# First group in two halves with mask products, staged loads, 768-column rows and reused tiles in a four-block stack

## The chip, the cores and the metric

The kernel runs on one core of one Trainium2 chip. The metric is the device time of one execution in microseconds, the median of several runs. All matrix work is in 32-bit floats.

## The reference

The input x is 8 sequences of 1024 rows of 256. Four blocks follow each other, each on the layer norm of x and added to x:

```python
x = x + linear_attention_layer(_layernorm(x))   # own two norms, gelu FFN 256 -> 1024 -> 256
x = x + relu_ffn(_layernorm(x))                 # 256 -> 1024 -> 256
x = x + softmax_attention(_layernorm(x))        # one head of 256, not causal
x = x + fp4_ffn(_layernorm(x))                  # silu(gate) * up, 256 -> 704 -> 256
```

The first block's attention has 16 heads of 16 columns and is causal. With q and k after a sigmoid, it computes per head and position

```python
sink_in  = normal / sum_d((q + EPS) * (cumsum(k) + EPS))
src_out  = normal / sum_d((k + EPS) * (cumsum(q) + EPS))
cons_sink = sum_d((q + EPS) * (cumsum(k * src_out) + EPS)) / normal
cons_src  = exp(clip(sum_d((k + EPS) * (cumsum(q * sink_in) + EPS)) / normal, -1, 1))
src_comp  = cons_src / cumsum(cons_src) * normal
x = (q * sink_in / normal) @ cumsum(outer(k, v * src_comp)) * sigmoid(cons_sink)
```

`normal` is the position from 1. In block 4 every 16 columns of the activations and weights are scaled by their largest size and rounded to the values of a 4-bit float before each product.

## The kernel before

**Tiling.** The rows are handled in chunks of 128, and four chunks (512 positions) make a group; a sequence has two groups, so there are 16 groups and 64 chunks. `linear_group` (L750) does the attention of block 1 for a group: `front` norms each chunk's x and turns it into `n0T`; q and k come as four tiles of 128 x 512 with columns of heads on the partitions; running sums along positions are scans on VectorE (`running`, L697), with the last column kept in `carry_cur` or `carry_w` for the next group. `head_sums` (L663) adds the 16 columns of each head with products against `hsum`, so that the four kinds of sum of all heads lie packed in one 128 x 128 tile (four chunks of 32 rows). On it the reciprocals and the exponential are done. To multiply q or k by such a packed factor it has to be repeated over the 16 columns of each head: `spread` (L678) writes the packed tile to DRAM and reads it back with each row repeated 16 times, one 128 x 512 tile for each of four parts. This is done for `flow` (four parts) and for `scale` (two parts, of q alone). `linear_chunk` (L897) then does v, the scores, the sum with the carried state `kv_sum`, the product with Wo, and the norm that gives h.

`dense` (L1070) runs both FFNs of a group half by half (256 rows), eight steps of 128 hidden columns each: a first product `half,w_ff`, the activation, and two steps later the second product `w_ff,hidden` into an accumulating bank. Each step's weights (two transfers of 128 KB) are loaded anew into five `w_ff` buffers. `norms_1` and `norms_2` follow each half. When all eight chunks of a sequence are through, `soft_chunk` (L1225) does blocks 3 and 4 for a chunk: the query product with `wqk`, scores against all keys (`n2T,qT`), exponential, transposes, product with `vt`, norm, rounding (`fp4`, L523), gate and up products (`wgT`, `wuT`), silu, rounding of the 704 columns of `hid`, six transposes (`hqT`) and the down product with `wdT`. The 704 columns are five tiles of 128 and one of 64:

```python
INTER_TILES = [(t * P, min(P, INTER - t * P)) for t in range((INTER + P - 1) // P)]
...
                lhsT=hqT[k // 4][:rows_, k % 4, :],
                rhs=wdT[:rows_, k, :],
```

**Order.** All parts are generators that say what they need next. The class `Plan` keeps an estimated time for each engine, tile, buffer and PSUM bank (`took`, L140, has the prices), and `run` (L231) always takes the part that could go on first, TensorE's work last among equals, then by due time (`at`). Every instruction is chained to the one before it on its engine (`Queue`, L255), so the order of this plan is the order on the chip, on all five engines. Times in the plan are not waited for on the chip: there an instruction waits for its operands and buffers alone. Because every instruction is issued through `Queue`, all have line L268 in the profile.

**Buffers.** `TILES` (L42) has the number of buffers of each kind: five `lin`, nine `flow`, seven `prob`, five `soft`, four `rows`, three `hid` and so on. [...]At most four chunks are in `soft_chunk` at a time, and at most two between their query product and their value product.

**Start.** Constants are made first, then the five `v_pad` tiles are cleared, four x chunks are loaded, then all weights and bias rows in one row on the sync engine's queue. The rounding of block 4's weights (`fp4_weights`: `w_raw`) and the product of block 3's query and key weights (`softmax_weights`: `wqk_raw`, `wqk_T`) are started at once and take turns with the first group.

Of the kernel before, what the change touches and what calls it, by code (L numbers as in the profile page):

```python
# [33 lines left out]
BANKS = 8  # L34
INTER_TILES = [(t * P, min(P, INTER - t * P)) for t in range((INTER + P - 1) // P)]
# [9 lines left out]
    "lin": (5, D, F32),  # L45
# [7 lines left out]
    "hid": (3, INTER, F32),  # L53
    "q_c": (2, INTER, BF16),
}


class Plan:
# [9 lines left out]
    def __init__(self, tc, nc):  # L68
        self.tc, self.nc = tc, nc
        self.free = {}  # L70
        self.done = {}
        self.by = {}
        self.banks = []
        self.live = {}
        self.slots = {}
        self.kind = {}
        self.used = {}
        self.held = set()
        self.kept = set()
        self.last = {}  # L80
        self.act_set = 0
        self.parts = []
        for name in ("tensor", "vector", "scalar", "gpsimd", "sync"):
            setattr(self, name, Queue(self, name))
# [19 lines left out]
    def take(self, kind, tile_):  # L104
        name = tile_.tensor.name
        slots, live = self.slots.setdefault(kind, []), self.live.setdefault(kind, set())
        if len(live) + len(slots) == TILES[kind][0]:
# [11 lines left out]

    def slot_free(self, kind):  # L120
        slots, live = self.slots.get(kind, []), self.live.get(kind, ())
        if len(live) + len(slots) < TILES[kind][0]:
            return 0.0
        return min(slots) if slots else None

# [5 lines left out]

    def bank_free(self, tag, n, count):
        banks = self.banks.get(tag, [])
        if len(banks) + count <= n:
            return 0.0
        times = sorted(self.used[b] for b in banks if b not in self.held)
        k = count - (n - len(banks)) - 1
        return times[k] if k < len(times) else float("inf")

    def took(self, queue, op, args, kw):  # L140
# [12 lines left out]
        if queue == "tensor":  # L153
# [4 lines left out]
            if op == "matmul" and (kw["lhsT"].shape[-1] <= 32 or kw["lhsT"].shape[0] <= 32):  # L158
                cost *= 0.25
            after = 0.2  # L160
        elif queue == "vector":
            each = {"reciprocal": 6.2e-3, "tensor_tensor_scan": 2.15e-3}.get(op, 1.05e-3)
            cost = 0.15 + each * size
        elif queue == "scalar":
            cost = 0.2 + 0.95e-3 * size
# [4 lines left out]
        elif queue == "gpsimd":  # L170
            cost = 0.4 + 1.3e-3 * size
        else:
            cost, after = 0.4, 2.2
# [7 lines left out]
        end = start + cost  # L181
        self.free[queue] = end
# [11 lines left out]
    def need(queue, tiles, banks=0, when=None, at=None, unused=(), fresh=None):  # L194
# [3 lines left out]
            queue=queue, tiles=tiles, banks=banks, when=when, at=at, unused=unused, fresh=fresh  # L198
# [14 lines left out]
    def ready(self, need):  # L213
# [8 lines left out]
        if need.fresh is not None:  # L222
            times.append(self.slot_free(need.fresh))
# [7 lines left out]
    def run(self):  # L231
        while self.parts:
            now = self.free.get("tensor", 0.0)
            best = None
            for part in self.parts:
# [3 lines left out]
                key = max(t - now, 0.0), part[1].queue == "tensor", part[2]  # L239
                if best is None or key < best[0]:  # L240
                    best = key, part
            assert best is not None, "every part waits for another"
            if best[0][0] > 0.0:
                self.free["tensor"] = now + best[0][0]
# [42 lines left out]
def block_stack_kernel(ctx: ExitStack, tc: tile.TileContext, a: dict, out: bass.AP):  # L287
# [51 lines left out]
    def make(kind, name=None):  # L339
        bufs, width, dtype = TILES[kind]  # L340
        t = wk.tile([P, width], dtype, tag=kind, name=name or kind, bufs=bufs)
# [11 lines left out]
    def load_row(name, width):  # L353
        t = const.tile([P, width], F32, tag=f"b_{name}", name=f"b_{name}")
        nc.sync.dma_start(out=t, in_=a[name].partition_broadcast(P))
        return t

    def load_tiles(name, width, kt):
        t = const.tile([P, kt, width], F32, tag=f"w_{name}", name=f"w_{name}")
        nc.sync.dma_start(out=t, in_=a[name].rearrange("(k p) n -> p k n", p=P))  # L360
        return t

    def load_cols(name, n):
        t = const.tile([P, n], F32, tag=f"c_{name}", name=f"c_{name}")
        nc.sync.dma_start(out=t, in_=a[name])
        return t


    ident = const.tile([P, P], F32, name="ident")
    make_identity(tc.nc, ident)  # L370
    triu = const.tile([P, P], F32, name="triu")
    make_upper_triangular(tc.nc, triu)
    bdiag = const.tile([P, P], F32, name="bdiag")
    make_block_diagonal(tc.nc, bdiag, DH)
    parity = const.tile([P, 2], F32, name="parity")
    nc.vector.tensor_reduce(
        parity, bdiag.rearrange("p (g e d) -> p e g d", e=2, d=DH), AX.XY, ALU.max
    )
    neghalf = const.tile([P, 1], F32, name="neghalf")
    nc.vector.memset(neghalf, -0.5)  # L380
    one = const.tile([P, 1], F32, name="one")
    nc.vector.memset(one, 1.0)

    hsum = const.tile([P, 4, 32], F32, name="hsum")
    nc.vector.memset(hsum, 0.0)
    for b in range(4):
        nc.vector.tensor_copy(
            hsum[:, b, 8 * b : 8 * b + 8], bdiag.rearrange("p (h d) -> p h d", d=DH)[:, :, 0]
        )

    pos_i = sm.tile([P, P], I32, tag="e", name="pos_i", bufs=1)
    for t in range(G):
        nc.gpsimd.iota(
            pos_i[32 * t : 32 * t + 32, :], pattern=[[1, P]], base=t * P + 1, channel_multiplier=0
        )
    pos = const.tile([P, P], F32, name="pos")
    nc.vector.tensor_copy(pos, pos_i)
    rpos = const.tile([P, NG, P], F32, name="rpos")
    for g in range(NG):
        nc.vector.tensor_scalar(rpos[:, g, :], pos, float(g * GT), None, ALU.add)  # L400
    nc.vector.reciprocal(rpos, rpos)
    row_i = const.tile([P, 1], I32, name="row_i")
    nc.gpsimd.iota(row_i, pattern=[[0, 1]], base=0, channel_multiplier=1)
    nc.vector.tensor_scalar(row_i, row_i, 16, None, ALU.bitwise_and)
    src = const.tile([P, 1], F32, name="src")
    nc.vector.tensor_copy(src, row_i)
    nc.vector.tensor_scalar(src, src, 1.0 / 16.0, None, ALU.mult)
    sink = const.tile([P, 1], F32, name="sink")
    nc.vector.tensor_scalar(sink, src, -1.0, 1.0, ALU.mult, ALU.add)
    sign = const.tile([P, 1], F32, name="sign")  # L410
    nc.vector.tensor_scalar(sign, src, 2.0, -1.0, ALU.mult, ALU.add)
    upper = const.tile([P, 1], F32, name="upper")
# [1007 lines left out]
```

## Time and profile before

| what | us |
|---|---|
| runs: median (lowest to highest of 3) | 2755.65 (2754.45 to 2756.18) |
| profiled execution, its own time | 2750.45 |
| its span, first to last instruction | 2748.6 |
| PE busy | 2614.9 (95%) |
| DVE busy | 1953.3 (71%) |
| ACT busy | 1219.6 (44%) |
| POOL busy | 597.7 (22%) |

The span is what the page's shares refer to; the execution's own time adds 1.85 us. PE is TensorE's products and transposes, DVE is VectorE, ACT is ScalarE, POOL is GpSimd, SP the sync engine that issues all transfers. A 32-bit product[...] stands twice in the counts of PE; a transpose stands once. Ends of matmuls are modelled, so that what a product costs is better read from the start of one to the start of the next.

### The profile page before, as it was taken

The numbers are of one execution on the slowest core, as the hardware profiler recorded it, in microseconds if no ns is written. First come the engines' busy times: TensorE is split into PE (matmuls) and PEld (weight loads), VectorE is DVE, ScalarE is ACT, GpSimd is POOL, SyncE is SP. The second block draws the span as 40 slices with busy tenths as digits, with TensorE's granted clock in tenths as the row PEclk, the third lists the DMA queues.
The fourth block names the chain that finished last, engine by engine and source line by source line (L and its number), as shares of the span: only waits on it lengthen the run. The fifth ranks groups of instructions, "written<-read, shape, count | busy, mean of one in ns | idle before, by whom it ended". The sixth has DMA issues, their size and how long they took to land.

```text
span 2748.6 us, 45646 instructions
## 1 busy us (share of the span) xinstructions
PE 2614.9 (95%) x16620; PEld 1998.1 (73%) x16620; DVE 1953.3 (71%) x4459; ACT 1219.6 (44%) x2453; POOL 597.7 (22%) x1100
## 2 busy tenths in 40 slices
PE   3888999999999999999999999999999999999997
PEld 1667677777777777777777777777777777877664
DVE  6877676685867778587776858768685777755565
ACT  2424344534554454444535354444545445353343
POOL 1323322121321312122221223213131222211000
PEclk7999999999999999999999999999999999999999
DMA  4234231322223232232222223222322313122000
GB/s 107 76 103 141 71 104 57 93 71 86 82 68 98 65 92 67 75 102 62 90 66 78 82 79 100 62 90 69 90 65 80 109 49 91 60 80 76 14 12 14
DMA packets 283215, 211.61 MB, mean 77 GB/s; under 512 B 23921, under 2 KB 270705, under 8 KB 282993
## 3 DMA queue, kind: packets, MB, share of 16 engines
q1 hardware_dynamic: 282992, 208.71, 25.5%
q8 instruction: 133, 2.18, 0.3%
q14 instruction: 90, 0.73, 0.1%
HBM read 189.74 MB, written 18.87 MB: 76 GB/s over the span
## 4 chain that ended last, share of the span: by engine, by line
PE 83%; DVE 11%; DMA 2%; ACT 2%; issue 1%; POOL 1%; SPq 0%; DVEq 0%; POOLq 0%; ACTq 0%
PE bank L268 83%; DVE hid L268 3%; DVE n L268 1%; DVE x_amax L268 1%; DVE ln_st L268 1%; DMA spread<-packed 1%; DVE mx L268 1%; DVE sc L268 1%; DVE prod L268 1%; ACT L268 1%; DMA w_ff<-in_L_ffn_w_dram 1%; SPq L268 0%; DVE u L268 0%; DVE x_r L268 0%; POOL ln_rstd L268 0%
## 5 line engine op out<-in xcount | busy, mean ns | idle before, releaser
L268 PE MATMUL bank<-half,w_ff 128*128 128x256 f32 x2048 | 533.8, 384 | 17.1 <-DMA w_ff<-in_L_ffn_w_dram 13.7
L268 PE MATMUL bank<-w_ff,hidden 128*128 128x256 f32 x2048 | 530.4, 384 | 3.4 <-ACT hidden L268 3.4
L268 PEld LDWEIGHTS bank<-half,w_ff 128*128 128x128 f32 x2048 | 382.8, 192 | 94.9 <-issue 32.3
L268 PEld LDWEIGHTS bank<-w_ff,hidden 128*128 128x128 f32 x2048 | 366.9, 191 | 76.4 <-issue 29.6
L268 ACT ACT_TABLE_LOAD x285 | 365.7, 1283 | 61.9 <-PE bank L268 54.6
L268 POOL TENSOR_SCALAR ln_ve<-ln_mv 128x1 f32<-128x1 f32 x384 | 102.4, 267 | 1110.1 <-DVE ln_mv L268 1099.6
L268 ACT ACTIVATE hidden<-bank,c_L_ffn_b 128x256 f32<-128x256 f32 x256 | 120.8, 472 | 320.5 <-PE bank L268 319.8
L268 PE MATMUL bank<-n2T,qT 128*128 128x512 f32 x512 | 243.9, 599 | 2.3 <-ACT qT L268 2.3
L268 POOL TENSOR_TENSOR ln_rstd<-ln_ve,neghalf 128x1 f32<-128x1 f32 x384 | 237.4, 618 | 32.0
L268 PE MATMUL bank<-vt,probT 128*128 128x256 f32 x1024 | 232.2, 380 | 0.0
L268 DVE TENSOR_TENSOR hid<-hid,bank 128x352 f32<-128x352 f32 x128 | 65.9, 518 | 229.4 <-PE bank L268 189.2
L268 PEld LDWEIGHTS bank<-vt,probT 128*128 128x128 f32 x1024 | 194.0, 190 | 38.1 <-issue 7.7
L268 DVE TENSOR_TENSOR sc<-bank,triu 128x512 f32<-128x512 f32 x256 | 162.3, 682 | 54.9 <-PE bank L268 54.9
L268 PE MATMUL bank<-wdT,hqT 128*128 128x256 f32 (+1 forms) x768 | 190.9, 390 | 0.8 <-ACT hqT L268 0.8
L268 ACT ACTIVATE hidden<-bank,c_L_attn_b 128x256 f32<-128x256 f32 x256 | 121.5, 474 | 146.3 <-PE bank L268 144.8
L268 POOL TENSOR_TENSOR xr<-xr,b_L_attn_ln_b 128x256 f32<-128x256 f32 x64 | 62.6, 996 | 531.3 <-DMA xr<-in_L_attn_inputs_dram 531.1
L268 PE MATMUL bank<-wgT,xqT 128*128 128x352 f32 x512 | 175.4, 465 | 1.4 <-ACT xqT L268 1.4
L268 PE MATMUL bank<-wuT,xqT 128*128 128x352 f32 x512 | 172.4, 459 | 0.0
L268 PEld LDWEIGHTS bank<-wdT,hqT 128*128 128x128 f32 (+1 forms) x768 | 139.7, 190 | 40.8 <-issue 20.2
L268 PEld LDWEIGHTS bank<-n2T,qT 128*128 128x128 f32 x512 | 92.7, 191 | 73.7 <-issue 62.5
L268 PEld LDWEIGHTS bank<-wuT,xqT 128*128 128x128 f32 x512 | 97.3, 190 | 54.1
L268 ACT ACTIVATE hid<-bank 128x352 f32<-128x352 f32 x128 | 59.3, 463 | 154.0 <-PE bank L268 152.6
(174 smaller groups left out, 4382.5 us busy)
## 6 DMA issues: line engine op xcount, KB each, us to landing
w_ff<-in_L_attn_W_dram SPq DMA_DIRECT2D x512, 128.0 KB
w_ff<-in_L_ffn_w_dram SPq DMA_DIRECT2D x512, 128.0 KB
spread<-packed SPq DMA_DIRECT2D x96, 256.0 KB
x<-in_L_attn_inputs_dram SPq DMA_DIRECT2D x64, 128.0 KB
xr<-in_L_attn_inputs_dram SPq DMA_DIRECT2D x64, 128.0 KB
rows<-res SPq DMA_DIRECT2D x64, 128.0 KB
rows<-rows SPq DMA_DIRECT2D x64, 128.0 KB
out_dram<-y SPq DMA_DIRECT2D x64, 128.0 KB
```

Of the source, the lines that this page charges most:

```text
L268: ins = method(*args, **kw)
```

## The change

The first group (p = 0) is computed as two spans of two chunks; all later groups have one span of four. In a span of two the spread is made by TensorE: the packed tile is multiplied with a mask of zeros and ones, and q and k are multiplied with the result in PSUM. The masks are made by ScalarE from the identity, in two `prob` buffers that are free at that time. Loads and constants are put in stages: x of the first two chunks, Wk and Wq come first; rows, FFN weights and block 3's and 4's weights come after the plan has reached a stage (`count["stage"]`). Block 4's rows get 768 columns with zeros at the end. After the last chunk of linear attention, `prob`, `soft` and `rows` tiles can also come from `flow`, `lin` and `x` buffers, q and k become two more `hid` buffers, eight chunks may be in `soft_chunk` instead of four, and three instead of two between query and value product. `lin` has four buffers instead of five. The state product of a chunk shares the bank of its attention product. The plan's prices are changed for all queues, a change of TensorE's tile shape gets a price, and a transfer's landing follows from its bytes; among parts that could go at once, the plan stays with small tiles when the last product was one of these.

```diff
+INTER_PAD = -(-INTER // P) * P
...
-    "lin": (5, D, F32),
+    "lin": (4, D, F32),
...
-    "hid": (3, INTER, F32),
+    "hid": (3, INTER_PAD, F32),
...
+SPARE = {"prob": "flow", "soft": "lin", "rows": "x"}
...
+            if tiled != self.tiled:
+                cost += 0.2
+            self.tiled = tiled
...
-            cost, after = 0.4, 2.2
+            cost = 0.4
...
+        if queue == "sync":
+            n = 4e-6 / 160e-3
+            for d in outs[0].shape:
+                n *= d
+            self.free["rings"] = max(self.free.get("rings", 0.0), end) + n
+            after = self.free["rings"] - end + 1.8
...
-                key = max(t - now, 0.0), part[1].queue == "tensor", part[2]
+                stays = self.tiled and part[1].tiled
+                wait = max(t - now - (0.3 if stays else 0.0), 0.0)
+                key = wait, part[1].queue == "tensor", not stays, part[2]
...
+    def load_weights_and_rows():
+        for i, (stage, label, t, src) in enumerate(loads):
+            yield dma(at=0.0, when=lambda: count["stage"] >= stage)
+            nc.sync.dma_start(out=t, in_=src)
...
+    xs = {c: load_x(c) for c in range(2)}
+    for i in (1, 0):
+        nc.sync.dma_start(out=wqkv[i], in_=wqkv_in[i])
...
+    def spread_near(packed, span, pairs):
+
+        yield pe(packed, *mask_tiles, banks=len(pairs))
+        out = {}
+        for pair in pairs:
+            bank = mm_bank()
+            for j, b in enumerate(pair):
+                mask = mask_tiles[b // 2][:, b % 2 * D : (b % 2 + 1) * D]
+                h = 32 * span.start
+                for t in range(2):
+                    nc.tensor.matmul(
+                        bank[:, j * D + t * P : j * D + (t + 1) * P],
+                        lhsT=mask[h : h + 64, t * P : (t + 1) * P],
+                        rhs=packed,
+                        start=True,
+                        stop=True,
+                    )
+                out[b] = bank[:, j * D : (j + 1) * D]
+            plan.keep(bank)
+        return out
...
+        spans = (range(0, 2), range(2, 4)) if p == 0 else (range(G),)
+        for span in spans[1:]:
+            plan.start(linear_span(p, span, fronts, tiles), p + 0.01)
+        yield from linear_span(p, spans[0], fronts, tiles)
...
-        weighted = yield from spread(flow, (2, 0, 3, 1))
+        if near:
+            weighted = yield from spread_near(flow, span, ((2, 0), (3, 1)))
+        else:
+            weighted = yield from spread(flow, (2, 0, 3, 1))
...
+        yield pe(when=lambda: count["linear"] == B * NCH)
+        plan.spare = True
+        for n in ("q", "k"):
+            h = kept([P, 2, GT], n, 1).rearrange("p k t -> p (k t)")
+            nc.gpsimd.memset(h[:, INTER:INTER_PAD], 0.0)
+            hids.append(h[:, :INTER_PAD])
+        plan.size["hid"] += 2
...
-            for k, (f0, rows_) in enumerate(tiles):
-                nc.tensor.transpose(bank[:rows_, k, :], hid[:, f0 : f0 + rows_], ident)
+            bank = turned([hid[:, f0 : f0 + P] for f0, _ in tiles])
...
-                lhsT=hqT[k // 4][:rows_, k % 4, :],
-                rhs=wdT[:rows_, k, :],
+                lhsT=hqT[k // 4][:, k % 4, :],
+                rhs=wdT[:, k, :],
...
-                when=lambda: q["normed"] == NCH and cc - count["out"] < 4 and "softmax" in weights,
+                when=lambda: q["normed"] == NCH and cc - count["out"] < (8 if plan.spare else 4) and "softmax" in weights and "ends" in late,
```

## The prediction

> **What bounds the kernel now.** I read the slices of the page first, because they say where the idle time lies.
>
> ```profile
> PE   3888999999999999999999999999999999999997
> PEclk7999999999999999999999999999999999999999
> ```
>
> TensorE is the bound, in order and nearly full, except in the first four slices of 68.7 us and the last. The busy time by stage puts numbers on this (columns: stage and its length, then busy us and instructions of PE, PEld, DVE, ACT, POOL, then clock, DMA share, GB/s).
>
> ```profile
> 0.00:100.00 100.00, 44.80 (x441) 30.54 (x445) 66.90 (x168) 22.36 (x58) 16.98 (x43) 0.81 0.31 83
> 100.00:200.00 100.00, 86.96 (x669) 69.03 (x665) 79.26 (x181) 39.37 (x91) 28.62 (x53) 0.95 0.37 112
> 200.00:300.00 100.00, 85.85 (x577) 68.87 (x569) 77.54 (x187) 37.79 (x87) 28.49 (x52) 0.93 0.38 112
> 300.00:400.00 100.00, 95.84 (x667) 74.12 (x656) 66.93 (x144) 45.05 (x85) 27.91 (x50) 0.97 0.32 95
> 400.00:2400.00 2000.00, 1988.48 (x12953) 1526.71 (x12951) 1467.39 (x3330) 936.05 (x1858) 461.75 (x838) 1.00 0.26 79
> 2540.00:2748.60 208.60, 175.16 (x725) 120.82 (x723) 122.96 (x279) 76.18 (x155) 10.54 (x22) 0.96 0.04 13
> ```
>
> PE idles 55.2 us in the first 100, 31.4 in the next 300, 11.5 in the 2000 of the middle and 33.4 in the last 208.6, after the last FFN weights. So time is won in two ways only: less PE work anywhere, or less idle time at the start and at the end. The chain of waits says what the start waits for (start, us, what):
>
> ```profile
> 45.56 2.53 DMA packed<-flow
> 48.10 3.77 DMA spread<-packed
> ...
> 70.90 2.44 DMA packed<-scale
> 74.04 4.66 DMA spread<-packed
> ```
>
> These two round trips through DRAM, 6.3 and 7.8 us from issue to the first product, stand in a chain of DVE work on the whole first group. The first FFN matmul comes at 98.07 in the timeline, the group's fourth transposed h at 109.57. The timeline of PE shows the third place, block 4's last product (start, us, form, count), against an ordinary x4 of 0.86 just before it:
>
> ```profile
> 2390.07 1.03 PE L268 MATMUL bank<-half,w_ff 128*128 128x256 f32 x4
> 2390.93 2.95 PE L268 MATMUL bank<-wdT,hqT 128*128 128x256 f32 x12
> 2393.81 0.44 PE L268 MATMUL bank<-ident,n 128*128 128x128 f32 x2
> ```
>
> From start to start the twelve passes take 2.88 us, twelve ordinary ones 3 x 0.864 = 2.59. The groups by form say which two are dear: the last tile has 64 rows.
>
> ```profile
> L268 PE MATMUL bank<-wdT,hqT 64*128 64x256 f32 x128 | 44.5, 428 | 0.0
> ```
>
> And at the very end the last chunk's fp4 work on DVE is bare:
>
> ```profile
> 2731.20 1.35 PE L268 MATMUL bank<-wuT,xqT 128*128 128x352 f32 x4
> 2739.82 1.51 PE L268 MATMUL bank<-ident,hid 128*128 128x128 f32 x6 [7.28 <-DVE hid L268]
> ```
>
> [...]from the start of one matmul to that of the next it is 0.09 us longer where the tile shape changes (0.309 for 0.216; the 0.29 us above is two changes and a pair that doesn't overlap, 0.320). [...]the clock falls to half. The trace agrees: 0.50 in 40 to 60 us, where PE is busy for 3 of 20. [...] ACT_TABLE_LOAD costs: 1.28 us; the page has 285 at a mean of 1283 ns.
>
> **Part A, 768 columns in block 4.** hid, hqT and wdT get zero rows, so all six tiles have 128 rows. Per chunk 2.88 - 2.59 = 0.29 us of PE; 64 chunks: **-18.4 us**. All lies on PE at its bound. Transposes stay six a chunk, and the 64-column one already takes as long as the others (279 ns both). The two hqT copies (263 + 262 ns) become one of 256 columns (370): 10 us off ACT, which is 44% busy, worth nothing. The new memsets (three hid tails, wdT, later two) are on POOL, 22% busy, under 0.2 us each by v_pad's 0.56 for eight times the width; one FFN step behind them covers it.
>
> **Part B, the start.** The first group's four chunks become two spans of two. A span's spread is made by mask matmuls in PSUM; of DMAs, 2 packs and 6 spreads go. I add the DVE order of the changed program, since DVE carries the chain. A 256-wide scan lies between 467 ns (128 wide) and 1.24 us (512): 0.73. So a flow step is 0.73 + 0.15 carry + 0.42 product = 1.33, a weighted one 1.75.
> - Constants, statistics and norms of x 0 and 1: now constants (3.3 to 8.7) come first and n at 10.8; with half of them put off, 7.8.
> - Rest of the constants, statistics of x 2 and 3: 3.0, to 10.8. k and q of the first span come by 10 to 13 (four 0.86 products, 0.47 sigmoids).
> - Four flow steps 5.3 and two norms 0.85: 16.9. Head sums 0.65, reciprocal 0.95, flow 0.3: 18.8.
> - Mask products: 4 matmuls, 8 passes. None is in the trace; the nearest is the 64-row tile, 0.22 for streaming 256 plus 0.1 for a load that doesn't overlap; for 128 columns 0.21, so 1.7 (0.9 if loads overlap[...]): 20.5. This replaces the 6.3 us trip.
> - Four weighted steps and, between them, the second span's flow steps, 7.0 + 5.3: 32.7. Then e, Exp, totals, reciprocals and scale, 5.6: 38.3; scale's products and q x2, then v: 43. Here the old kernel is at 80.
> - Scores of two chunks, attention, the second span's remaining weighted steps and scale, two norms (DVE 20): first FFN matmul at about **63** instead of 98.
> - Two more chunks (eight sc at 0.68, norms, six weight operations; DVE 20): fourth h at about **85** instead of 109.6.
>
> By then PE has done one first and two second FFN steps more than before (+2.6 us), but not six w_raw tiles and the softmax weights (-5): 24.5 - 2.5 = 22. Those weights now fall beside group 0's FFN, where DVE was 79% busy; six tiles at some 2.9 us of DVE are 17 us in a 100-us stretch with 21 free. I take 2 back: **-20 us**, 8 to 32.
>
> Queues: SP issues x 0, x 1, Wk, Wq first (0.47 each); the rows used later and five FFN weight tiles follow in its list, under 3 MB, at the 191 GB/s of the first 20 us some 15 us, so in well before 63. PE's new wait for flow has the second span's last q product and head sums behind it; DVE needs them two steps later. POOL now waits for bo before its res adds; v_pad memsets are behind them, needed at 43. ACT does eight mask copies (0.37) before n0T, between ident (under 3 us) and 8. All covered; if not, up to 3 us. Fourteen more table loads are 18 us on ACT, covered by its 56% idle.
>
> **Part C, the end.** After linear attention, its flow, lin, x, q and k tiles serve block 3 and 4; eight chunks may be under way instead of four. Both orders have ten last products left after the last FFN matmul. What changes is distance: chunk 62's scores were followed by one product (2.9 us) before its probabilities were transposed; now by that, 0.9 of wqk and 1.7 of scores. Exp needs 0.7 + 0.2 + 1.3 + 1.4 = 3.6, so those waits go; the fp4 waits (DVE hid) go in part. The 7.28 above and the closing 3 us stay. Of 33.4 idle, 10.3 stay for certain; of 23 I take **-14** (0 to -23).
>
> **Part D, the middle.** The planner's prices change, so the whole order changes. Changes of tile shape outside block 4: 288 before, 292 now, 0.4 us. Idle is 0.6% there; a gain is at most 11 us. A loss is open: lin has four buffers for five. I take 0, -5 to +12.
>
> **Sum.** 18.4 + 20 + 14 = 52.4. The profiled execution took 2750.45 (span 2748.6 and 1.85 around it), so 2698; the median shown is 5.2 higher, so 2755.65 - 52.4 = **2703**.
>
> **Rivals.**
> 1. *The early start isn't kept.* FFN weights are 256 KB per 1.73 us of PE, 151 GB/s; from 140 to 160 us DMA moved 146, and PE waited 7.21 us for w_ff. If groups 0 and 1 run at the rate of transfers, an earlier start only meets that wall sooner: 2755.65 - 32.4 = 2723. Against it: 31.4 us in 300 is all the idle there was.
> 2. *The end doesn't shorten*, since the last chunk's chain sets it and the deeper lead comes too late: 2755.65 - 38.4 = 2717. For it: the last five PE steps stand in the same order.
> 3. *Slower: lin with four buffers.* v, k, kv, xo, u and h of a chunk share it; a chunk's v then waits for the u or h of the one before, and PE, in order, stands behind v's bank. The price is per chunk, on 60 chunks: above 52.4 / 60 = 0.87 us each the change loses. At 1.3 (POOL's ve and rstd 0.9 and h 0.5): +78 - 52 = +26, 2781. Against: PE waited 1.2 us in all before the Wo products.
> That the change doesn't do what it says: the changed program's list has the 24 mask matmuls and no 64-row wdT; this is excluded.
>
> **How the numbers follow.** Forecast 0.53, first rival 0.18, second 0.20, third 0.09. Likeliest 2703. The bounds of B, C and D, taken independent, are about 18 up or down; rivals 1 and 2 lie inside that, and the upper end goes part of the way to rival 3: 2676 to 2737. A difference of 0.2%, 5.5 us, is what can be told from none: faster 0.90, the same 0.02, slower 0.08 (the third rival but for its cheap end).
>
> **What would show it.** A: wdT x12 in 2.6 us, no 64-row group. B: first half,w_ff near 63, fourth ident,h near 85, no packed in the first 100 us; PE idle in 0 to 400 near 67, not 87. C: the stretch after the last w_ff near 190 us. D: idle in the middle near 12. It is wrong if PE waits for lin's readers, for w_ff beyond 20 us, or for w_raw, or if the mask products take over 4 us a span.

## The result and the profile after

The kernel after takes **2747.74 us** (median of 8 runs, 2744.89 to 2751.26), the kernel before on the same chip 2754.80 (8 runs, 2749.19 to 2756.76): a ratio of 0.9977, 95% interval 0.9967 to 0.9988. It is faster by 7 us where 52 were forecast, and 2747.74 lies 11 us above the range. The profiled execution took 2751.26 (span 2749.6), while the one of before, at 2750.45, was a short one among its runs; so the two traces below differ by only +1.0 us of span, and 8 us of what the medians show aren't in them.

PE's busy tenths in the slices of the page after:

```profile
PE   6988999999999999999999999999999999999897
```

The first slice rose from 3 to 6. The busy time by stage, in the columns that the prediction named, shows what happened later:

```profile
0.00:100.00 100.00, 73.64 (x587) 55.48 (x588) 80.22 (x207) 31.32 (x76) 27.05 (x64) 0.83 0.30 78
100.00:200.00 100.00, 87.79 (x698) 68.44 (x697) 84.12 (x195) 39.53 (x95) 31.68 (x52) 0.95 0.37 106
200.00:300.00 100.00, 90.80 (x718) 71.16 (x717) 86.08 (x213) 36.17 (x92) 27.89 (x55) 0.98 0.38 113
300.00:400.00 100.00, 98.36 (x571) 74.22 (x570) 74.90 (x157) 49.03 (x97) 23.66 (x41) 1.00 0.36 106
400.00:2400.00 2000.00, 1969.14 (x12793) 1523.38 (x12792) 1458.56 (x3293) 954.50 (x1816) 429.71 (x833) 1.00 0.27 78
2540.00:2749.60 209.60, 175.66 (x714) 124.75 (x712) 121.88 (x278) 63.56 (x134) 11.76 (x22) 0.93 0.04 13
```

PE idles 49.4 us in the first 400 instead of 86.5 (67 were predicted), but 30.9 in the middle 2000 instead of 11.5, and 33.9 in the last stage, which is not shorter. The landmarks of the start, from PE's timeline (start, us, form, count), first of the kernel before, then of the kernel after:

```profile
98.07 1.13 PE L268 MATMUL bank<-half,w_ff 128*128 128x256 f32 x4 [0.24 <-ACT half L268]
...
109.57 0.41 PE L268 MATMUL bank<-ident,h 128*128 128x128 f32 x2 [0.85 <-DVE h L268]
```

```profile
75.67 1.03 PE L301 MATMUL bank<-half,w_ff 128*128 128x256 f32 x4
...
94.22 0.38 PE L301 MATMUL bank<-ident,h 128*128 128x128 f32 x2
```

The first FFN product starts at 75.7 instead of 98.1, the transpose of the fourth h at 94.2 instead of 109.6. Block 4's last product, in the same view, takes 2.59 us from start to start, and no tile of 64 rows is left:

```profile
2531.02 2.75 PE L301 MATMUL bank<-wdT,hqT 128*128 128x256 f32 x12
2533.61 1.03 PE L301 MATMUL bank<-w_ff,hidden 128*128 128x256 f32 x4
```

So the edits do locally what they say. The gain is lost to waits. The longest items of PE's waits in the middle (400 to 2400; what PE waited for, then total us, times, longest), first of the kernel before, then of the kernel after:

```profile
PE bank L268 <- DVE u L268: 3.7, 6, 0.6
PE bank L268 <- ACT hidden L268: 3.4, 6, 0.6
...
```

```profile
PE bank L301 <- DVE y L301: 8.6, 7, 1.4
PE bank L301 <- ACT prob L301: 4.5, 6, 0.9
...
PE bank L301 <- DVE res L301: 2.7, 2, 2.2
...
```

One wait of the largest item of after shows how it comes about. The two timelines around it, PE first, then DVE:

```profile
1340.30 1.03 PE L301 MATMUL bank<-w_ff,hidden 128*128 128x256 f32 x4
1342.56 1.13 PE L301 MATMUL bank<-half,w_ff 128*128 128x256 f32 x4 [1.23 <-DVE y L301]
```

```profile
1340.16 1.28 DVE L301 TENSOR_TENSOR_SCAN prod<-one,carry_w,spread 128x512 f32<-128x512 f32 x1
1341.47 0.69 DVE L301 SCALAR_TENSOR_TENSOR prod<-k,prod 128x512 f32<-128x512 f32 x1
1342.08 0.42 DVE L301 TENSOR_TENSOR y<-bank,rows 128x256 f32<-128x256 f32 x1
```

PE wants a PSUM bank that DVE reads in `y`, 0.42 us of work; but DVE works through a group's weighted steps back to back (from 1330 on, with two norms between them), and `y` stands behind the last of them. DVE isn't overloaded (73% busy in the middle, as before). It has the wrong instruction next.

**A table for all runs.** For each trace I split every distance from the start of one matmul to the start of the next into the usual one for that pair of tile shapes (the median in the traces of before and after) and the rest. The first, summed, is PE's own work; the rest is waiting, which includes what products lose at a reduced clock (0.83 granted in after's first 100 us). What lies ahead of the first matmul's start (11.3 us before, 7.0 after) and behind the last one's (3.5 in both) is in neither. Pairs that occur once only make the sums uncertain by 2 to 3 us. Counting the closely packed small products in another way shifts some 20 us from PE's own work into the waits in every row, most of it in the middle, so differences between rows are uncertain by up to 6. The split is that of the profiled execution, which took between 8 us less (e1) and 6 us more (e12) than the median beside it. All times in us.

| kernel | time, median | PE's own work | waits 0-400 | waits 400-2400 | waits after 2400 |
|---|---|---|---|---|---|
| before | 2754.8 | 2554 | 98 | **35** | 46 |
| after | 2747.7 | 2558 | 63 | **62** | 56 |
| e1 part A alone, planned anew | 2768.4 | 2537 | 98 | 58 | 51 |
| e5 part A alone, order kept | 2736.7 | 2537 | 100 | 36 | 46 |
| e9 after without part A, order kept | 2763.4 | 2574 | 60 | 58 | 55 |
| e3 after, five lin | 2748.7 | 2558 | 62 | 63 | 55 |
| e4 after, no reuse at the end | 2757.1 | 2558 | 62 | 63 | 65 |
| e2 after, old prices, old choice | 2728.1 | 2558 | 76 | 48 | 36 |
| e12 e2 without the reuse | 2736.7 | 2558 | 75 | 49 | 49 |
| e6 after, old choice only | 2738.8 | 2556 | 61 | 66 | 46 |
| e7 after, old prices only | 2780.8 | 2554 | 78 | 105 | 39 |
| e10 before, one price 0.16 | 2801.8 | 2556 | 92 | **93** | 43 |
| e11 after, one price 0.16 | 2743.7 | 2553 | 53 | 65 | 56 |
| e16 e2, one price 0.16 | 2766.3 | 2555 | 76 | **80** | 41 |
| e8 e2, no rounding of weights | 2772.5 | 2554 | 70 | 94 | 47 |
| e15 e2, first group in one span | **2720.7** | 2540 | 89 | 44 | 39 |

Each kernel was compared with the kernel before on its own chip, whose median there was 2752.8 to 2754.8.

### The profile page after: what moved, and what is told of

Same layout as the page of the kernel before. It is cut to its first block, busy times and chain, and to the rows that moved or that the text cites. A ratio compares the mean times of both kernels' runs of the same rounds, so it can differ in the third digit from the quotient of the medians.

```text
span 2749.6 us, 45693 instructions
## 1 busy us (share of the span) xinstructions
PE 2631.4 (96%) x16687; PEld 2025.0 (74%) x16687; DVE 1976.4 (72%) x4509; ACT 1235.2 (45%) x2421; POOL 569.9 (21%) x1106
## 4 chain that ended last, share of the span: by engine, by line
PE 63%; DVE 26%; ACT 3%; issue 2%; DMA 2%; POOL 2%; SPq 0%; DVEq 0%; ACTq 0%
PE bank L301 63%; DVE hid L301 4%; DVE prod L301 4%; DVE n L301 3%; DVE ln_st L301 2%; DVE x_amax L301 2%; DVE spread L301 1%; DVE u L301 1%; DVE mx L301 1%; DVE x_r L301 1%; POOL ln_rstd L301 1%; ACT L301 1%; DVE res L301 1%; DVE ln_mv L301 1%; ACT q_c L301 1%
## 5 line engine op out<-in xcount | busy, mean ns | idle before, releaser
L301 PE MATMUL bank<-w_ff,hidden 128*128 128x256 f32 x2048 | 537.1, 385 | 0.3 <-DVE u L301 0.2
L301 POOL TENSOR_SCALAR ln_ve<-ln_mv 128x1 f32<-128x1 f32 x384 | 95.6, 249 | 1599.7 <-DVE ln_mv L301 1589.2
L301 POOL TENSOR_TENSOR ln_rstd<-ln_ve,neghalf 128x1 f32<-128x1 f32 x384 | 230.2, 600 | 32.0
L301 DVE TENSOR_TENSOR hid<-hid,bank 128x352 f32<-128x352 f32 x116 | 59.9, 517 | 224.5 <-PE bank L301 200.0
L301 PE MATMUL bank<-wdT,hqT 128*128 128x256 f32 x768 | 180.6, 386 | 1.3 <-ACT hqT L301 1.3
L301 PEld LDWEIGHTS bank<-wdT,hqT 128*128 128x128 f32 x768 | 147.9, 194 | 24.6 <-ACT hqT L301 2.6
L301 PEld LDWEIGHTS bank<-wuT,xqT 128*128 128x128 f32 x512 | 98.1, 192 | 56.6 <-issue 1.8
L301 PE MATMUL bank<-ident,n 128*128 128x128 f32 x512 | 99.8, 282 | 24.9 <-DVE n L301 19.4
L301 PEld LDWEIGHTS bank<-wgT,xqT 128*128 128x128 f32 x512 | 94.3, 192 | 38.9 <-issue 6.4
```

Of the source, the lines that this page charges most:

```text
L301: ins = method(*args, **kw)
```

## The experiments

**Part A and the order (e1, e5, e9).** Two versions give the kernel before its 128-row tile (the last tile overlaps the one ahead by 64 columns, and their weight rows are zero). e1 has one hqT copy as in after, and its plan comes out reordered; e5 keeps both ACT copies, and with them the order of every engine (POOL alone has one memset more). e9 takes the 128 rows out of after, with its order kept.

```diff
-                lhsT=hqT[k // 4][:rows_, k % 4, :],
-                rhs=wdT[:rows_, k, :],
+                lhsT=hqT[k // 4][:, k % 4, :],
+                rhs=wdT[:, k, :],
...
 # e1 only
-            if half == 0:
-                nc.scalar.copy(hqT[0], bank)
-            else:
-                for k, (f0, rows_) in enumerate(tiles):
-                    nc.scalar.copy(hqT[1][:rows_, k, :], bank[:rows_, k, :])
+            nc.scalar.copy(hqT[half][:, : len(tiles), :], bank)
```

> The kernel before with block 4's sixth tile made of 128 rows and nothing else (the last tile overlaps the fifth by 64 columns, whose rows of wdT are zero; five lin buffers, old plan). If PE's work is the bound all through, 64 x 0.29 = 18.4 us go and it takes about 2736. If the plan's order has a second bound just behind PE, whose waits take the gain back, it stays at 2750 to 2755, with wdT x12 at 2.59 us all the same.

> The kernel before with one edit: the sixth tile of the gated product's down product takes 128 rows (it overlaps the fifth by 64 columns, whose weight rows are zero), written so that the planned order of every engine's instructions is the one of before. TensorE's own work falls by 64 x 0.29 us = 18 us. Theory 'order' (the PE work counts in full where the order stays; it was only a reshuffled order that cost the first such kernel 27 us of waits): 2737 +- 4 us, PE's stalls near those of before. Theory 'second bound' (vector and scalar results stand just behind PE in every order, so PE waits as soon as it gets faster): 2748 or more, the sequence period stays at 323 to 325 us and the waits for DVE and ACT results grow by 10 us or more.

> The kernel after with the sixth tile of the gated product's down product at 64 rows again, the planned order of every engine unchanged. Theory 'the PE work of part A counts in full in this order too, and was not what was lost': 2748 + 18 = 2766 us, +-4. Theory 'in the order of after PE waits for others, so that its work is partly hidden' (PE's waits in 400 to 2400 are twice those of before): +5 to +12, 2753 to 2760.

Measured: e1 **2768.39** (7 runs, ratio 1.0041, 1.0029 to 1.0052), e5 **2736.68** (4 runs, 0.9936, 0.9922 to 0.9951), e9 2763.38 (7 runs, 1.0035, 1.0022 to 1.0047). The same edit is worth -18.1 us in the kept order, +14 in the reordered one (which neither of my two theories for e1 allowed), and its removal from after costs 15.6. PE's own work moves by 17 us each time; in e5 the waits stay as they were, in e1 22 us of new ones come in the middle. Most are in two items of e1's waits from 400 to 2400:

```profile
PE bank L268 <- DVE n L268: 12.8, 6, 2.5
PE bank L268 <- ACT prob L268: 10.8, 17, 1.2
```

A sequence of two groups, which takes 323.7 us from first FFN product to first FFN product before, takes 321.5 in e5: eight chunks at 0.288 less. This also refutes the idea that I had ahead of e5, that a second bound stands right behind PE.

**Buffers and the end (e3, e4, e12).** e3 gives `lin` its fifth buffer back (and takes hid's tail columns to make room). e4 and e12 leave out the reuse at the end and the depth of eight, in after and in e2.

```diff
-        plan.spare = True
-        for n in ("q", "k"):
-            h = kept([P, 2, GT], n, 1).rearrange("p k t -> p (k t)")
-            nc.gpsimd.memset(h[:, INTER:INTER_PAD], 0.0)
-            hids.append(h[:, :INTER_PAD])
-        plan.size["hid"] += 2
```

> The changed kernel with five lin buffers; for room, block 4's tile of 128 rows is made by overlap as in e1, and hid has 704 columns. Theory 2 (lin): 2720 to 2730, the middle's waits gone. Theory 1 (prices and choice): 2743 to 2750, as the changed kernel.

> The changed kernel without the reuse of flow, lin, x, q and k tiles at the end, four chunks under way. If the reuse brings what it was counted for, 2755 to 2762 (the end 10 to 14 us longer). If the end is set by the last chunks' own chain, 2745 to 2750. If the reuse itself costs (deeper lead puts DVE work of later chunks ahead of what PE needs), 2735 to 2742.

> The kernel after with old prices and old choice of the plan (2728 us) and without the reuse of linear attention's tiles at the end, four chunks under way. The plan up to the last linear group is nearly the same, so this shows what the reuse does at the end in this order. If the reuse is the cause of the short end (193 us after the last weight-tile product for 208): 2740 to 2745, the end back at 205 to 210. If the order is the cause: 2728 +- 4.

Measured: e3 2748.66 (15 runs, 0.9976, 0.9968 to 0.9984), the same as after; so four `lin` cost nothing (the order stays nearly the same: 84 of DVE's 4509 places differ). e4 2757.12 (12 runs, 1.0015, 1.0007 to 1.0024): the reuse is worth 9.4 us. e12 2736.73 (4 runs, 0.9943, 0.9928 to 0.9958): it is worth 8.6 in the other order (I had given 2740 to 2745, or 2728 if the order did it). The waits after 2400 fall by 9 to 13 us with it in both pairs, and the middle stays, so this is the reuse itself.

**The plan (e2, e6, e7, e10, e11, e16).** Each has the instructions of the kernel that it changes, but for ACT's table loads and the choice of reused tiles, in another order. e2 has after's edits with both the prices and the choice of before; e6 takes back the choice alone (with it the price of a change of tile shape), e7 the other prices alone. e10, e11 and e16 change one number, in before, after and e2.

```diff
 # e6; in e2 also the prices
-                stays = self.tiled and part[1].tiled
-                wait = max(t - now - (0.3 if stays else 0.0), 0.0)
-                key = wait, part[1].queue == "tensor", not stays, part[2]
+                key = max(t - now, 0.0), part[1].queue == "tensor", part[2]
 # e10, e11, e16
-            cost = 0.15 + each * size
+            cost = 0.16 + each * size
```

> The changed kernel with the old prices and the old choice in the plan. Theory 1, the new prices and the stay at small tiles make an order in which PE waits some 4 us more per sequence (mostly for DVE): this one takes 2712 to 2725, with the middle's idle time back near 12 us. Theory 2, the four lin buffers: no better than 2745, waits as in the changed kernel.

> The kernel after with its new prices in the plan, but the choice between parts as before (no staying on a small tile shape, no 0.2 us for a switch of the tile, TensorE's planned time moved only by a wait). If the choice rule is what costs the kernel after its end: near 2728 us, last weight-tile product near 2534 us and the rest near 193 us, as with old prices and old choice together. If the prices of the engines and transfers are what costs it: near 2748.

> The kernel after with the prices of before for VectorE, ScalarE, GpSimd and transfers, but the new choice between parts and the price of a tile switch. If the prices cost the 20 us: near 2728 us. If the choice costs them: near 2748. If each costs half, both of this pair come near 2738; if any reshuffled order moves the time by so much, the pair does not add up.

> The kernel before with one number of its plan changed: the fixed part of a VectorE price 0.16 instead of 0.15 us. No instruction is added, removed or made longer; only the order in which the parts are put into the queues changes, in some thousand places. Theory 'the order alone is worth tens of us' (the orders seen so far had 35 to 105 us of PE waits between 400 and 2400, and before has the least of them): 2755 to 2785, with more PE waits in the middle than the 35 us of before. Theory 'the order hardly matters; each edit has its own cost': within 5 us of 2755.

> The kernel after with the same number of the plan changed, 0.16 for 0.15 us. Theory 'the order alone is worth tens of us': anywhere between 2725 and 2785, over 5 us from 2748, and the difference lies in PE's waits, not in its work. Theory 'order hardly matters': within 5 us of 2748.

> The kernel after with old prices and old choice (2728 us) and the fixed part of VectorE's price 0.16 instead of 0.15. No instruction is changed. Theory 'the order alone is worth tens of us': over 5 us from 2728, PE's work near 2558 us again and the difference in its waits. Theory 'order hardly matters in this version': within 5 us.

Measured: e2 **2728.1** (4 runs, 0.9900, 0.9884 to 0.9917), e6 2738.75 (0.9937, 0.9920 to 0.9955), e7 2780.83 (1.0100, 1.0083 to 1.0116). Against after, the old choice alone brings 9 us, the old prices alone cost 33, both together bring 20: they don't add, so neither is a cost of its own. And one hundredth of a microsecond in one price moves before by **+48.5 us** to 2801.78 (from 2753.24 on its chip; 4 runs, 1.0175, 1.0160 to 1.0190), e2 by +38 to 2766.28 (1.0052, 1.0032 to 1.0072) and after by -4 to 2743.73 (0.9965, 0.9952 to 0.9977), which is hardly clear of the noise and, by what I had put down for e11, speaks for an order that hardly matters. PE's own work is the same within 5 each time. My range for e10 ended at 2785, too low, and e2 came 3 us above its range. PE is busy for 1948.2 us of e10's middle, against 1988.5 in before. Over all the orders in the table the waits there lie between 35 and 105 us; those of before, and of e5, which keeps its order, are the lowest. An edit that makes the plan choose anew leaves that order. ACT's table loads change with the order too, but not with the time: e10 has 13 more than before and is slower, e16 has 45 fewer than e2 and is slower as well.

**The start (e8, e15).** e15 is e2 with its first group in one span, through DRAM again; the staged loads and late constants stay. e8 is e2 without the rounding of block 4's weights.

```diff
 # e15
-        spans = (range(0, 2), range(2, 4)) if p == 0 else (range(G),)
+        spans = (range(G),)
 # e8
-            yield from fp4(raw, width, rows)
```

> The kernel after with old prices and old choice of the plan (2728 us), with the first group as one span whose spreads go through DRAM again (the staged loads stay). If the two spans with mask products are worth the start: the first FFN product at 90 us or later instead of 74.5, and the time up by 10 to 20, to 2738 to 2748. If the staged loads and constants brought the start: below 2735. Since this too reorders the plan, PE's waits between 400 and 2400 (48 us in the base) have to be read beside it.

> The kernel after with the plan's old prices and old choice, and the rounding of the gated product's weights left out (the raw weights are turned instead: VectorE's share of this weight work is gone, its PE turns stay). Theory 'displaced vector work' (half of the early start is lost between the first and second group because VectorE's weight rounding, moved out of the start, falls into that group's FFN): the time from group 0's first FFN product to group 1's falls from 120 to near 110 us, and the whole by about as much, to near 2718. Theory 'nothing to do with it' (PE's own work and the order of products set this interval): it stays at 117 to 121 us and the whole at 2725 to 2730.

Measured: e15 **2720.70** (4 runs, 0.9879, 0.9862 to 0.9895), the fastest kernel of this study: 27 us faster than after, and 32 below before on the same chip. The first 100 us of e2, then of e15 (columns as above):

```profile
0.00:100.00 100.00, 75.06 (x595) 57.37 (x596) 77.95 (x206) 31.21 (x78) 27.75 (x64) 0.83 0.30 81
```

```profile
0.00:100.00 100.00, 57.18 (x522) 40.36 (x523) 69.00 (x170) 30.51 (x70) 26.57 (x64) 0.81 0.37 97
```

PE is less busy without the spans, and its first FFN product comes later (81.2 for 74.5). Yet e15's timeline has the fourth h at 90.9, ahead of e2 (93.7) and of after:

```profile
81.24 1.13 PE L284 MATMUL bank<-half,w_ff 128*128 128x256 f32 x4 [0.24 <-ACT half L284]
...
90.90 0.38 PE L284 MATMUL bank<-ident,h 128*128 128x128 f32 x2
```

Group 1's first FFN product comes at 193.6 in e15 and 195.9 in e2. So most of the earlier start is there without the spans (17 of e2's 24 us at the first FFN product), and I put it down to the staged loads. The two spans bring 6.8 us at that product, which are gone one group later: they add 15 us of PE busy time (2612.0 against 2596.9 on the pages), 10 of it in the mask products. In this order they pay for nothing; since leaving them out reorders the plan as well, the 7 us between e15 and e2 aren't theirs alone (4 lie in the middle's waits). In before PE waited 8.4 us of the first 100 for `wqk_raw` from DRAM; e15's list of waits there has no such item.

e8 came out at 2772.46 (4 runs, 1.0068, 1.0053 to 1.0083), outside both of its ranges, because its new order waits more in the middle (94 us). Its start still answers the question: DVE is busy for 128 us from 100 to 300 instead of 154 in e2, and group 1's first FFN product comes 123 us after group 0's, instead of 121. So DVE's rounding isn't what stretches this interval (110 in before); what does is open.

**What a bad order waits for (e13, e14, e17, e18).** In e10 the trace shows a wait of 7 us of DVE, and two of PE after it. DVE's timeline, then PE's:

```profile
1865.33 0.29 DVE L268 SCALAR_TENSOR_TENSOR flow<-pos,r 128x128 f32<-128x128 f32 x1
1872.61 0.69 DVE L268 TENSOR_TENSOR spread<-k,spread 128x512 f32<-128x512 f32 x1 [6.99 <-DMA spread<-packed]
```

```profile
1884.67 0.43 PE L268 MATMUL bank<-prod,hsum 128*32 128x128 f32 x8 [2.33 <-DVE prod L268]
1885.02 2.71 PE L268 MATMUL bank<-wgT,xqT 128*128 128x352 f32 x4
...
1903.29 2.08 PE L268 MATMUL bank<-half,w_ff 128*128 128x256 f32 x4 [3.26 <-DVE u L268]
```

DVE's queue has the product with the spread right behind `flow`, so it stands for the whole round trip through DRAM (6.99 us), and all that stands behind it is late. e13 (and its control e14, in before's order) lets the spreads read what the first group packed. e17 (control e18) leaves the transfer out from the fourth group on, so the factors have no effect there. The order of PE, DVE, ACT and POOL is kept in each.

```diff
 # e13, e14
+            flat = firsts[kind] = hbm.tile([32, GT], F32, tag="packed0", name="packed0", bufs=2)
...
-                    tensor=flat.tensor,
-                    offset=flat.offset + 8 * b * GT,
+                    tensor=x.tensor,
+                    offset=x.offset + 8 * b * GT,
...
+                for x in (firsts[kind], flat)
...
+            nc.sync.dma_start(out=t, in_=old)
 # e17, e18
+            if p < 3:
+                nc.sync.dma_start(out=t, in_=wide)
...
-            nc.vector.tensor_tensor(w, cur[b], w, ALU.mult)
+            nc.vector.tensor_tensor(w, cur[b], w if p < 3 else cur[b], ALU.mult)
```

> The kernel before with the reordered plan (VectorE's fixed price 0.16, 2802 us), every engine's order kept, but the wide spreads of all groups after the first read what the first group left in DRAM, so they no longer wait for their own group's pack (the values of flow and scale are then the first group's). This takes the pack's 2.4 us out of each round trip on which VectorE's in-order queue stands (12 waits of 3.7 us between 400 and 2400, and in the trace PE's 2.3 and 3.3 us waits follow 7.0 us of one). Theory 'a round trip at the head of VectorE's queue is what this order pays for': PE's waits in the middle fall from 93 to 60 us or less, and the time by 25 to 40, to 2762 to 2777. Theory 'the cost is spread over many places in the queues': it falls by under 10 us, to 2792 or more.

> The same edit in the kernel before with its own order, as the control (flow and scale of the groups after the first are then the first group's). VectorE waits as long for spreads here (12 waits, 41.9 us) while PE waits for little. Theory 'round trip at the head of the queue': in this order enough PE work stands beside each wait, so the time falls by at most 8 us in the middle, and by the pack waits of groups 1 and 2 at the start, to 2743 to 2753. Theory 'spread over many places': the same small fall as in the reordered kernel.

> The kernel before with the reordered plan (VectorE's fixed price 0.16, 2802 us), every engine's order kept, but from the fourth group on the wide spreads are not transferred at all: VectorE multiplies q and k by themselves where it multiplied by the spread (flow and scale have no effect there). The pack stays. The earlier attempt took under 1 us from each round trip (VectorE's waits for spreads went from 43.8 to 40.8 us), so it did not test the theory; here these waits are gone. Theory 'a round trip at the head of VectorE's in-order queue is what this order pays for': PE's waits for u and prod (27 us of the 49 listed between 400 and 2400) go, and the time falls by 20 to 40, to 2762 to 2782. Theory 'the cost is spread over many places in the queues': these waits come from other work ahead in the queue, and the time falls by under 10, to 2792 or more.

> The same edit in the kernel before with its own order, as the control (flow and scale have no effect from the fourth group on). Theory 'round trip at the head of the queue': this order has PE work beside each of its 12 waits for a spread (41.9 us of VectorE, 10 us of PE waits listed), so the time falls by under 6 us, to 2748 to 2754. Theory 'spread over many places': the same, so that the pair is told apart by the reordered kernel; a fall of over 15 here would say that spreads cost in every order.

Measured: e13 2795.21 (4 runs, 1.0149, 1.0134 to 1.0164) and e14 2748.42 (14 runs, 0.9984, 0.9976 to 0.9992): 7 and 4 us less. This pair tells nothing, since DVE's waits for spreads only went from 43.8 to 40.8 us. e17 came to **2776.21** (4 runs, 1.0079, 1.0064 to 1.0094), 25.6 below e10, and e18 to 2745.09 (7 runs, 0.9971, 0.9957 to 0.9985), 8.5 below before, where I had expected under 6. The bad order pays 17 us more for the spread transfers than the good one, of the 48 that lie between them. Not all of it need be DVE's standing: 5.2 us of e10's listed waits after 300 us are for FFN weights, and they too are gone when the spreads leave the queue. The two largest items left in e17's waits from 400 to 2400:

```profile
PE bank L269 <- DVE u L269: 17.5, 8, 3.5
PE bank L269 <- ACT prob L269: 6.1, 10, 1.5
```

I had expected the waits for u to go with those for prod; they stayed. e17's timelines show why, PE first (its product before ended at 1881.9):

```profile
1885.39 1.84 PE L269 MATMUL bank<-half,w_ff 128*128 128x256 f32 x4 [3.47 <-DVE u L269]
```

```profile
1882.79 0.89 DVE L269 TENSOR_TENSOR hid<-hid,x_s 128x704 f32<-128x704 f32 x1
1883.60 0.68 DVE L269 TENSOR_REDUCE mx<-bank 128x1 f32<-128x512 f32 x1
...
1884.94 0.39 DVE L269 TENSOR_TENSOR u<-bank,res 128x256 f32<-128x256 f32 x1
```

Here the rounding of a chunk of block 4 and a softmax maximum stand ahead of `u`, which reads the FFN's accumulating bank and so lets the next FFN half begin. Of the rest of e10's cost, about 30 us, this is a part.

Another part is the clock. Right after the first of e10's waits shown above, the `wgT` product takes 2.51 us from start to start, where the same form takes 1.18 in after (2537.29 to 2538.47). In e10's middle the granted clock stands at half in seven stretches, 34 us in all (mean of the middle 0.99), and each follows a wait of PE of 2.1 to 4.2 us; in before's and e18's middle there is none (mean 1.00). I estimate from these 34 us that the half clock costs up to 17, and with the 40 us by which PE's idle time grew (51.8 for 11.5) this about makes up the 57 us (before rounding) between the two rows of the table. By this estimate such waits were paid twice in e10, once as idle time and once as slow products behind them (two further waits there, of 2.3 and 2.6 us, have no slow stretch behind them). In e17 it is still 20 us at half clock (mean 0.99). What else stands in the rest I haven't separated.

## Why the prediction was wrong

The parts of the sum against the two traces (after less before; waits from the table, unrounded):

| | predicted | measured |
|---|---|---|
| A, PE work | -18.4 | -17.6 (e5's own work; -18.1 in its time) |
| B, start | -20 | waits 0-400 and ahead of the first matmul -38.7; PE work for it and the rest +21.2 (uncertain by 6); together -17.5 |
| C, end | -14 | waits after 2400 +10.0 |
| D, middle | 0 (-5 to +12) | waits 400-2400 **+26.2** |
| sum | -52.4 | +1.1 in these two traces; -7 in the medians |

**D is the step that failed.** It makes 26 of the 53 us between the two sums, and C another 24. D read the middle's 0.6% idle as "a gain is at most 11 us" and bounded the loss by one mechanism, `lin`. Both ends looked at resources, and e3 shows that `lin` was not short. What the runs show in its place: the little idle time of before is a property of its order, and the new orders had 44 to 105 us of waits where before has 35. The sentence "The planner's prices change, so the whole order changes" was in the text, and a range of -5 to +12 didn't follow from it: e10 alone is +57 in the middle. Of the 26, 19 are idle time of PE. That the order can do this is shown; no run has after's edits in before's order of the middle, so that order is the whole of the 26 is not. One edit to the middle was taken back by no run, the bank that the state product shares: PE's listed waits for its reader `kv` are 1.0 us in after and 7.2 in e2.

**A was right, with a condition that it didn't state.** The 18.4 us are there to within 0.3 where the order is kept (e5) and within 3 in after's order (e9). "All lies on PE at its bound" holds only if the plan keeps its order, and in e1 a new one turned -18 into +14.

**B's sum was near by luck.** The chain of DVE steps put the first FFN product at 63, and it came at 75.7; h at 85, and it came at 94.2. Half of the delay was there when the first span's `flow` was done: its mask products start at 25.4 instead of 18.8. (A slip in the sum is small beside this: 0.73 + 0.15 + 0.42 is 1.30 for a flow step, not 1.33.) I charged the mask products as 1.7 us in a chain and left their and the smaller tiles' PE work out of the sum, which e15 against e2 puts at 15 to 18 us. The masks alone take 9.8 us in after, 4.9 a span, which is over the 4 that were named as a sign of being wrong. What made up for both is idle time: 37 us less in the first 400, where the text counted on 20. The net gain came with the staged loads and late constants, which I had let stand for 3 us of an earlier n: without the spans, e15 has some 14 us less waiting than before up to 400 us (what lies ahead of the first matmul counted in); the spans take off some 13 more, and their work takes that back. The 2 us for displaced weights were no issue in the way I meant it: with that DVE work gone (e8), the interval stayed.

**C's mechanism was right, its size was not, and its place was taken.** "Those waits go" was said of the probabilities: PE's listed waits for them after 2540 fell from 8.4 to 4.6 us, 2.6 under `prob` and 2.0 under `flow`, whose tiles hold probabilities there. That the fp4 waits "go in part" failed. In before they are one line of that list; in after the same waits come under the names of the reused tiles:

```profile
PE bank L268 <- DVE hid L268: 14.4, 5, 7.3
PE bank L268 <- ACT prob L268: 8.4, 6, 3.8
```

```profile
PE bank L301 <- DVE hid L301: 7.8, 3, 4.8
PE bank L301 <- DVE k L301: 7.3, 1, 7.3
PE bank L301 <- DVE q L301: 4.5, 1, 4.5
...
PE bank L301 <- ACT prob L301: 2.6, 2, 2.2
PE bank L301 <- ACT flow L301: 2.0, 1, 2.0
```

The waits for `hid`, `k` and `q` add up to 19.6 for 14.4. The reuse is worth 9 us in two orders, not 14 (e4, e12); after's order, without it, has 19 us more waits after 2400 than before (65 for 46), and that took it back. In e2 these waits are 11 us less than in before. The +10 is only in small part idle time, which rose by 2 us after 2400: the granted clock stands at half for 34 us there, for 18 in before (means 0.95 and 0.98), and I estimate from the 16 us more that they lose up to 8.

**The rivals.** The first was half right in its outcome and wrong in its reason: of the 22 us of lead at group 0's FFN, 12 are left at group 1's and 17 at group 2's, but the two waits of PE for FFN weights there, 7.2 and 6.5 us in before, are 6.5 and 4.3 in after. The second was right that the end wouldn't shorten, but not by the last chunk's chain: the reuse does shorten it (e4, e12). The third is refuted by e3. No rival spoke of the order.

The lower end of the stated range, 27 us below its middle, doesn't follow from the "about 18" given for it; this changes nothing here.

Open: which places in the queues make up the rest of a bad order, and whether a plan whose prices were nearer to the measured durations would find a good one; after's prices, which were meant to be nearer, didn't.

## What to carry to other kernels

Where a program writes the order of the queues, an edit has two effects, its work and a new order, and the second can be the larger one: run the edit once with the old order kept, and run the old kernel once with a meaningless change of the plan, to learn what a new order is worth. An engine that is 99% busy says that this order hides all else, not that other orders will. A wait for an engine that is 73% busy is a question of what stands ahead in its queue, and the timeline of that engine, read back from the late instruction, names it.

## What the runs showed that I had not expected

The time of one kernel moved by 48 us, 1.75%, with no instruction of the program changed (e10), and by the estimate above up to 17 of them are the half clock behind the new waits. And a wait can be large and free: e18 takes all 41.9 us of DVE's waits for spreads out of before's middle, and the whole kernel gets 8.5 us faster, some 6 of them between 300 and 400 us, where the waits fall from 7.6 to 1.9.
